# A convolution and a score layer on one core: each load cut in two and put behind a quarter of the output, on one queue

## The chip, the cores and the metric

The kernel runs on one core of one Trainium2 chip. The metric is the time of one execution on the device in microseconds (us); of several runs the median is given.

## The reference

Two layers on `x` of shape (4, 64, 256, 256), in float32. Batch is `b`, channel `c`, and each of the 256 (batch, channel) images is 256 x 256.

```python
# layer 0: a long convolution in two dimensions, whose kernel is an outer product
k = einsum('ijk,imk->ijmk', hx, hy)[0]       # hx, hy: small sine networks times a decay, (1, 256, 64)
k = transpose(k, (2, 0, 1))                  # one 256 x 256 kernel per channel, of rank one
y = irfft2(rfft2(x, s=(512, 512)) * rfft2(k, s=(512, 512)) / 512, s=(512, 512))[..., :256, :256]
x = y + x * bias[:, None, None]

# layer 1: weighted scores of the rows with each other, then a normalization per channel
scores = einsum('bpsd,bptd->bpst', x, x) / sqrt(256)
red = sum(scores * weights[None], axis=-1, keepdims=True)
y = x + red
y_hat = (y - mean(y, axis=(0, 2, 3))) * rsqrt(var(y, axis=(0, 2, 3)) + 1e-5)
out = y_hat * gamma[None, :, None, None] + beta[None, :, None, None]
```

## The kernel before

The work is one loop over the 64 channels; one pass of it handles all four images of a channel and is called a period here. The convolution kernel is of rank one, so the convolution is done as two multiplications with Toeplitz matrices, one along each axis. `toep` holds both Toeplitz matrices of a channel. The four images of a channel stand side by side as 64 x 64 blocks, so that every matmul uses a quarter of the array (64 rows, 64 columns).

The stages of a channel, by function:

- `conv_rows(c, u)` (matmuls on line L165) multiplies half `u` of `xin`, the input in the order that this product needs, with `toep`; it fills two PSUM tiles. `copy_rows` (L174, ScalarE, here ACT) copies them to `z`.
- `conv_cols(c, z)` (matmuls L189) makes the second product. VectorE (DVE) adds `x * bias` from `xt`, a second copy of the input in the output's order, and writes `x0` (L196).
- `gram(c, v)` (matmuls L221) makes the scores of two images. `weigh` (L234, L238) multiplies them with the weights `w` and sums; `spread` (L245, ACT) and `all_sum` (L250 on DVE, then L251, a sum over all partitions on GpSimd, here POOL) bring the row sums into the layout of `x0`. `pick_red` (L258, ACT) and `add_red` (L263, DVE) add them.
- `part_stats` and `stats` (L270, L276, L279) take mean and variance, `root` (L285 to L292) the standard deviation on ACT and POOL, `scale_shift` (L296 to L304, DVE) the factor and the offset.
- `finish` (L312, ACT) applies them and stores the result.

The order of the instructions on each engine is the order in which the program is written (`manual_schedule`). The main loop is software-pipelined: pass `c` works on `conv_cols` and `gram` of channel `c`, on `conv_rows` of `c + 1`, on `all_sum` and `add_red` of `p = c - 1`, on the statistics of `q = c - 2`, and on `finish` of `f = c - 3`.

All loads are issued on the queue of SyncE (SP): at the head of pass `c` come `load_w(c + 2)` (256 KB, L73), `load_xt(c + 2)` (1 MB, L68), `load_x(c + 3)` (1 MB, L63) and `load_h(c + 3)` (two DMAs of 128 KB for `toep`, L136, which wait until `conv_cols(c)` has read the buffer). The stores are issued on the queue of ACT, two of 512 KB in a period, each right behind its activation (L313). Load buffers are threefold (pool `ld`), `o` twofold, `x0` fourfold.

Before the loop a small network on 128 partitions makes `hx` and `hy` of all channels (L109 to L125); the result is written to DRAM (`g_dram`), from where `load_h` reads the Toeplitz matrices. The loads of channels 0 to 2 are issued around this.

On PE each matmul is preceded by its own weight load (PEld in the profile), both from one instruction stream.

## Time and profile before

| | |
|---|---|
| Three runs | 1023.18, 1023.28, 1025.0 us; median 1023.28 |
| Profiled execution | 1023.52 us; span from first to last instruction 1021.7 us |
| TensorE matmul (PE) busy | 923.9 us, 90%, 21,512 instructions |
| Weight loads (PEld) busy | 822.4 us, 80%, 21,512 instructions |
| DVE / ACT / POOL busy | 782.5 us (77%) / 519.5 us (51%) / 441.9 us (43%) |
| DMA | 238.70 MB, mean 234 GB/s; queue q1 (SP) 51.1%, q10 (ACT) 16.8% of 16 engines' time |
| Mean granted TensorE clock | 0.986 |

The profile is of one execution. An engine's busy time is the time in which one of its instructions ran; a line number such as L189 is a line of the kernel, and `x<-xt,p` says which tile is written from which. The chain that ended last follows the work back from the last instruction, at each step to what released it. "Issue" is time in which an engine stood still although the profile shows nothing that it waited for. A wait is listed as who waited, for what, the total in us, how often, and the longest. Stretches ("windows") give the busy time of each engine between two moments. A queue's share is the time that its packets took, over the time of all 16 DMA engines.

### The profile page before, as it was taken

The page shows a single profiled execution, that of the slowest core. Times are in us where ns is not written, and L with a number is a line of the kernel's source. Part 1 is how long each engine was busy: PE and PEld are TensorE (multiplying, and loading weights), DVE is VectorE, ACT ScalarE, POOL GpSimd, SP SyncE. Part 2 cuts the span into 40 slices and gives each one's busy share as a digit, 9 for nine tenths or more (in the row PEclk, how much of TensorE's full clock was granted, in tenths as well). Part 3 has the DMA queues.
Part 4 walks back from the last instruction along what each step waited for, and adds up shares of the span by engine and source line. Part 5 has one row for each costly group of instructions (what it writes and reads, how often), then busy time and mean ns, then how long its engine had stood idle before and what let it go on. Part 6 is the DMA issues. An engine that isn't in the chain of part 4 may idle for free.

```text
span 1021.7 us, 47771 instructions
## 1 busy us (share of the span) xinstructions
PE 923.9 (90%) x21512; PEld 822.4 (80%) x21512; DVE 782.5 (77%) x1878; ACT 519.5 (51%) x1029; POOL 441.9 (43%) x196
## 2 busy tenths in 40 slices
PE   2999999999999989999999999999999999999980
PEld 1888889898888978888878888889888888888870
DVE  2368778887777977887878787788787888778794
ACT  0245455455455545555545555545554554554554
POOL 0045345345345535534534543544453454454353
PEclk9999999999999999999999999999999999999995
DMA  7667587677577768677767677867776876776523
GB/s 209 192 199 253 204 270 246 227 255 267 202 259 237 260 231 283 233 243 260 249 208 270 223 246 259 276 226 242 274 238 212 279 246 218 265 241 246 190 85 123
DMA packets 65699, 238.70 MB, mean 234 GB/s; under 512 B 7446, under 2 KB 24536, under 8 KB 49112
## 3 DMA queue, kind: packets, MB, share of 16 engines
q1 hardware_dynamic: 46284, 167.89, 51.1%
q10 hardware_dynamic: 19212, 67.76, 16.8%
q8 instruction: 169, 2.77, 1.1%
q14 instruction: 34, 0.28, 0.1%
HBM read 168.05 MB, written 67.31 MB: 230 GB/s over the span
## 4 chain that ended last, share of the span: by engine, by line
PE 89%; issue 5%; DVE 3%; DMA 1%; POOL 1%; ACT 1%; POOLq 0%; ACTq 0%; DVEq 0%
PE g L221 34%; PE p L189 28%; PE p L165 27%; DMA toep<-g_sb 1%; POOL rd L251 1%; DVE x L263 0%; DVE bst L270 0%; PE ph L109 0%; DVE junk L234 0%; DVE x L196 0%; DVE fa L118 0%; ACT o L312 0%; DVE pr L238 0%; DMA fw_sb<-in_fw 0%; DVE fa L111 0%
## 5 line engine op out<-in xcount | busy, mean ns | idle before, releaser
L251 POOL PARTITION_ALL_REDUCE rd<-sp x64 | 391.8, 6122 | 425.3 <-DVE r L296 366.1
L221 PE MATMUL g<-x 64*64 64x256 f32 (+1 forms) x8192 | 376.2, 325 | 39.9 <-issue 38.1
L221 PEld LDWEIGHTS g<-x 64*64 64x64 f32 x8192 | 320.0, 133 | 82.7 <-issue 54.6
L165 PEld LDWEIGHTS p<-toep,xin 64*64 64x64 f32 x8192 | 296.5, 134 | 27.3 <-issue 12.4
L165 PE MATMUL p<-toep,xin 64*64 64x256 f32 (+3 forms) x8192 | 309.1, 298 | 10.1 <-DMA toep<-g_sb 7.3
L189 PE MATMUL p<-z,toep 64*64 64x256 f32 x5120 | 306.9, 377 | 8.0 <-issue 7.7
L189 PEld LDWEIGHTS p<-z,toep 64*64 64x64 f32 x5120 | 241.9, 133 | 47.0 <-issue 13.7
L234 DVE SCALAR_TENSOR_TENSOR junk<-g,w 128x256 f32<-128x256 f32 x256 | 107.1, 418 | 179.7 <-PE g L221 179.4
L312 ACT ACTIVATE o<-x,sh,g 128x1024 f32<-128x1024 f32 x128 | 159.0, 1242 | 149.3 <-DVE sh L304 122.3
L245 ACT ACTIVATE sp<-eye_sb,red 128x128 f32<-128x128 f32 x256 | 98.0, 397 | 202.5 <-DVE junk L234 202.0
L196 DVE SCALAR_TENSOR_TENSOR x<-xt,chan_sb,p 128x512 f32<-128x512 f32 x256 | 173.8, 740 | 19.4 <-PE p L189 19.4
L174 ACT COPY z<-p 128x512 f32<-128x512 f32 x256 | 136.2, 591 | 89.0 <-PE p L165 72.1
L270 DVE BATCH_NORM_STATS2 bst<-x 128x6 f32<-128x512 f32 x256 | 157.8, 678 | 0.0
L263 DVE TENSOR_TENSOR x<-x,rd 128x1024 f32<-128x1024 f32 x128 | 150.5, 1217 | 3.1 <-ACT rd L258 3.1
L238 DVE SCALAR_TENSOR_TENSOR pr<-g,w 128x256 f32<-128x256 f32 x256 | 107.6, 420 | 0.0
L288 POOL PARTITION_ALL_REDUCE tot<-mv x64 | 25.3, 396 | 119.2 <-ACT mv L287 119.2
L250 DVE TENSOR_TENSOR sp<-pr 128x512 f32<-128x512 f32 x64 | 44.3, 692 | 2.2
L258 ACT COPY rd<-rd 64x512 f32<-64x512 f32 x64 | 39.3, 615 | 5.8 <-POOL rd L251 4.3
L279 POOL PARTITION_ALL_REDUCE tot<-mv x64 | 24.7, 386 | 26.7 <-DVE mv L276 26.7
L290 ACT ACTIVATE r<-tot,eps 128x1 f32<-128x1 f32 x64 | 18.9, 295 | 32.8 <-POOL tot L288 32.8
L287 ACT ACTIVATE mv<-d,mv 128x1 f32<-128x1 f32 x64 | 24.8, 387 | 2.1
L299 DVE TENSOR_SCALAR u<-v,r 128x1 f32<-128x1 f32 x64 | 17.5, 273 | 7.0
(31 smaller groups left out, 161.6 us busy)
## 6 DMA issues: line engine op xcount, KB each, us to landing
xin<-in_x SPq DMA_DIRECT2D x64, 1024.0 KB, 9.7
xt<-in_xT SPq DMA_DIRECT2D x64, 1024.0 KB, 5.5
out<-o ACTq DMA_DIRECT2D x128, 512.0 KB, 8.5
w<-in_wl SPq DMA_DIRECT2D x64, 256.0 KB, 2.7
toep<-g_dram SPq DMA_DIRECT2D x126, 128.0 KB, 10.1
fw_sb<-in_fw ACTq DMA_DIRECT2D x1, 192.0 KB, 2.7
g_dram<-g_sb SPq DMA_DIRECT2D x1, 192.0 KB
decay_sb<-in_decay ACTq DMA_DIRECT2D x1, 128.0 KB, 5.6
```

What stands on the lines that cost most here:

```text
L165: nc.tensor.matmul(p1[i][half, j, H * k :], lhsT=xin[rows, k, u, j, half], rhs=toep[rows, 0, : S - H * k], start=(k == 0), stop=(k == 3),)
L174: nc.scalar.copy(zs[c][:, 2 * i : 2 * i + 2, u, :], p1[i])
L189: nc.tensor.matmul(p2[v][bass.ts(u, H), n, :], lhsT=toep[rows, 1, bass.ts(i - j, H)], rhs=z[rows, j, u, :], start=(j == 0), stop=(j == i),)
L196: nc.vector.scalar_tensor_tensor(x0[:, v, part], xt[:, v, part], chan_sb[:, 0, c : c + 1], p2[v], ALU.mult, ALU.add,)
L221: nc.tensor.matmul(gs[u][bass.ts(h, H), cols, :], lhsT=x0[rows, v, i, first + H * h : first + H * h + H], rhs=x0[rows, v, i, first:], star ...
L234: nc.vector.scalar_tensor_tensor(junk, g[:, 0:2, :], 1.0 / math.sqrt(S), w[:, 0:2, :], ALU.mult, ALU.mult, accum_out=red0[:, b : b + 1],)
L238: nc.vector.scalar_tensor_tensor(pr[:, b], g[:, 1:3, :], 1.0 / math.sqrt(S), w[:, 2:4, :], ALU.mult, ALU.mult)
L245: nc.scalar.activation(sp[:, b, 0, :], eye_sb, AF.Identity, scale=red0[:, b : b + 1])
L251: nc.gpsimd.partition_all_reduce(rd.rearrange("p b s -> p (b s)"), sp.rearrange("p b k s -> p (b k s)"), P, RED.add)
L263: nc.vector.tensor_tensor(x0[:, v], x0[:, v], r, ALU.add)
L270: nc.vector.bn_stats(bst[:, 2 * m + h, :], x0[:, m, 2 * h : 2 * h + 2])
L312: nc.scalar.activation(o[:, v], st8[c][0][:, v], AF.Identity, bias=sh, scale=g)
```

## The change

- `xin` and `xt` become two tiles each, with a DMA of 512 KB each; the arrays in DRAM are laid out so that each half is contiguous.
- The output is made in four parts per channel: `finish` handles one (128 x 512 elements), and each is stored with a DMA of 256 KB, on SP's queue and no longer on ACT's. The output array's layout follows; `o` has four buffers of a quarter.
- The four parts are put at four places of the period on ACT: ahead of `conv_cols`, between the two halves of `conv_rows`, between the two halves of the old `root` (now `spreads` and `root`), and after `gram(c, 0)`.
- Behind each store SP issues a load: a half of `xin`; the other half and `toep`; a half of `xt`; the other half and `w`. `xt` is loaded three channels ahead and no longer two.

The instructions of PE, DVE and POOL, and their order, stay as they are.

```diff
-    def load_x(c):
-        xin = ld.tile([P, 4, 2, 2, P], F32, tag="xin", name=f"xin_{c}")
-        nc.sync.dma_start(xin, x[c])
-        xs[c] = xin
+    def load_x(c, u):
+        xin = ld.tile([P, 4, 2, P], F32, tag=f"xin{u}", name=f"xin_{c}_{u}")
+        nc.sync.dma_start(xin, x[c, u])
+        xs[c, u] = xin
...
-    def root(c, mv, tot):
+    def spreads(c, mv, tot):
...
         nc.gpsimd.partition_all_reduce(tot[:, 1:2], mv[:, 2:3], P, RED.add)
+        return d
+
+    def root(c, tot):
+
         r = sm.tile([P, 1], F32, tag="r", name=f"r_{c}")
...
-    def finish(c, g, sh):
-        o = wk.tile([P, 2, 4, S], F32, tag="o", name=f"o_{c}")
-        for v in range(2):
-            nc.scalar.activation(o[:, v], st8[c][0][:, v], AF.Identity, bias=sh, scale=g)
-            nc.scalar.dma_start(out[c, :, v], o[:, v])
+    def finish(c, g, sh, v, n):
+        part = bass.ts(n, 2)
+        o = wk.tile([P, 2, S], F32, tag="o", name=f"o_{c}_{v}_{n}", bufs=4)
+        nc.scalar.activation(o, st8[c][0][:, v, part], AF.Identity, bias=sh, scale=g)
+        nc.sync.dma_start(out[c, v, n], o)
...
     for c in range(C + 3):
         p, q, f = c - 1, c - 2, c - 3
-        if c + 2 < C:
-            load_w(c + 2)
-            load_xt(c + 2)
-        if c + 3 < C:
-            load_x(c + 3)
-            load_h(c + 3)
         if 0 <= p < C:
             spread(p, 2)
             spread(p, 3)
             all_sum(p)
         if f >= 0:
-            finish(f, *scale_shift(f, *scales.pop(f)))
+            fin = (f, *scale_shift(f, *scales.pop(f)))
+            finish(*fin, 0, 0)
+        if c + 3 < C:
+            load_x(c + 3, 0)
         if c < C:
             begin(c)
             conv_cols(c, zs.pop(c))
         if 0 <= q < C:
-            sums[q] = stats(q, part_stats(q))
+            mv, tot = stats(q, part_stats(q))
         if c + 1 < C:
             begin_rows(c + 1)
-            for u in range(2):
-                copy_rows(c + 1, u, conv_rows(c + 1, u))
+            copy_rows(c + 1, 0, conv_rows(c + 1, 0))
+        if f >= 0:
+            finish(*fin, 0, 1)
+        if c + 3 < C:
+            load_x(c + 3, 1)
+            load_h(c + 3)
+        if c + 1 < C:
+            copy_rows(c + 1, 1, conv_rows(c + 1, 1))
         if 0 <= p < C:
             pick_red(p)
         if 0 <= q < C:
-            scales[q] = root(q, *sums.pop(q))
+            d = spreads(q, mv, tot)
+        if f >= 0:
+            finish(*fin, 1, 0)
+        if c + 3 < C:
+            load_xt(c + 3, 0)
+        if 0 <= q < C:
+            scales[q] = (d, *root(q, tot))
         if c < C:
             gram(c, 0)
             spread(c, 0)
             spread(c, 1)
+        if f >= 0:
+            finish(*fin, 1, 1)
+        if c + 3 < C:
+            load_xt(c + 3, 1)
+        if c + 2 < C:
+            load_w(c + 2)
         if 0 <= p < C:
             add_red(p, 0)
             add_red(p, 1)
```

`load_xt` is cut as `load_x` is; the loads before the loop follow (`x` and `xt` of channels 0 to 2 in halves, `xt` of channel 2 now before the loop).

More of the change, by code (lines that the diff above doesn't have):

```diff
@@ L59, in conv_scores_bn_kernel, with load_xt @@
     xs, xts, ws, hs = {}, {}, {}, {}
-    def load_x(c):
-        xin = ld.tile([P, 4, 2, 2, P], F32, tag="xin", name=f"xin_{c}")
-        nc.sync.dma_start(xin, x[c])
-        xs[c] = xin
-    def load_xt(c):
-        xt = ld.tile([P, 2, 4, S], F32, tag="xt", name=f"xt_{c}")
-        nc.sync.dma_start(xt, xT[c])
-        xts[c] = xt
+    def load_x(c, u):
+        xin = ld.tile([P, 4, 2, P], F32, tag=f"xin{u}", name=f"xin_{c}_{u}")
+        nc.sync.dma_start(xin, x[c, u])
+        xs[c, u] = xin
+    def load_xt(c, v):
+        xt = ld.tile([P, 4, S], F32, tag=f"xt{v}", name=f"xt_{c}_{v}")
+        nc.sync.dma_start(xt, xT[c, v])
+        xts[c, v] = xt
     def load_w(c):
@@ L95, in conv_scores_bn_kernel @@
     nc.vector.memset(g_sb[:, :P], 0.0)
-    load_x(0)
-    load_xt(0)
-    load_w(0)
-    load_x(1)
-    load_xt(1)
+    for c in range(2):
+        load_x(c, 0)
+        load_x(c, 1)
+        load_xt(c, 0)
+        load_xt(c, 1)
+        if not c:
+            load_w(c)
     g_dram = dram.tile([P, GW], F32, name="g_dram")
@@ L155, in conv_rows @@
     def conv_rows(c, u):
-        xin, toep = xs[c], hs[c]
+        xin, toep = xs.pop((c, u)), hs[c]
         p1 = [ps.tile([P, 2, S], F32, tag="ps", name=f"p1_{c}_{u}_{i}") for i in range(2)]
@@ L166, in conv_rows @@
                         p1[i][half, j, H * k :],
-                        lhsT=xin[rows, k, u, j, half], rhs=toep[rows, 0, : S - H * k],
+                        lhsT=xin[rows, k, j, half], rhs=toep[rows, 0, : S - H * k],
                         start=(k == 0), stop=(k == 3),
@@ L176, in conv_cols @@
     def conv_cols(c, z):
-        xt, toep, x0 = xts.pop(c), hs.pop(c), st8[c][0]
-        xs.pop(c)
+        xt = [xts.pop((c, v)) for v in range(2)]
+        toep, x0 = hs.pop(c), st8[c][0]
         for m in range(2):
@@ L196, in conv_cols @@
                 nc.vector.scalar_tensor_tensor(
-                    x0[:, v, part], xt[:, v, part], chan_sb[:, 0, c : c + 1], p2[v],
+                    x0[:, v, part], xt[v][:, part], chan_sb[:, 0, c : c + 1], p2[v],
                     ALU.mult, ALU.add,
@@ L292, in root @@
         nc.scalar.activation(v, tot[:, 1:2], AF.Identity, bias=eps, scale=1.0 / P)
-        return d, v, r
+        return v, r
     def scale_shift(c, d, v, r):
@@ L307, in scale_shift @@
         return g, sh
-    def finish(c, g, sh):
-        o = wk.tile([P, 2, 4, S], F32, tag="o", name=f"o_{c}")
-        for v in range(2):
-            nc.scalar.activation(o[:, v], st8[c][0][:, v], AF.Identity, bias=sh, scale=g)
-            nc.scalar.dma_start(out[c, :, v], o[:, v])
+    def finish(c, g, sh, v, n):
[3 more added lines that the diff above has]
+        nc.sync.dma_start(out[c, v, n], o)
     load_h(1)
     load_w(1)
-    load_x(2)
+    load_x(2, 0)
+    load_x(2, 1)
     load_h(2)
+    load_xt(2, 0)
+    load_xt(2, 1)
     def begin_rows(c):
@@ L401 @@
     arrays = {
-        "x": xi.transpose(2, 5, 4, 3, 0, 6, 1, 7).reshape(C, P, 4, 2, 2, P),
-        "xT": xo.transpose(2, 0, 5, 1, 4, 3).reshape(C, P, 2, 4, S),
+        "x": xi.transpose(2, 0, 5, 4, 3, 6, 1, 7).reshape(C, 2, P, 4, 2, P),
+        "xT": xo.transpose(2, 1, 0, 5, 4, 3).reshape(C, 2, P, 4, S),
         "wl": wl,
@@ L420 @@
     ]
-    o = nc.dram_tensor("out", (C, P, 2, 4, S), F32, kind="ExternalOutput").ap()
+    o = nc.dram_tensor("out", (C, 2, 2, P, 2, S), F32, kind="ExternalOutput").ap()
     with tile.TileContext(nc) as tc:
@@ L424 @@
     r = run_bass_kernel_spmd(nc, [arrays], core_ids=[0])
-    y = r.results[0]["out"].reshape(C, 2, H, 2, 4, S)
-    return np.ascontiguousarray(y.transpose(1, 3, 0, 5, 4, 2).reshape(B, C, S, S))
+    y = r.results[0]["out"].reshape(C, 2, 2, 2, H, 2, S)
+    return np.ascontiguousarray(y.transpose(3, 1, 0, 6, 2, 5, 4).reshape(B, C, S, S))
```

## The prediction

> **What bounds the kernel now.** I read the chain that ended last first, then TensorE's waits, then stretches of one channel each, then single waits in the timeline, then the DMA queues.

> ```profile
> ## 4 chain that ended last, share of the span: by engine, by line
> PE 89%; issue 5%; DVE 3%; DMA 1%; POOL 1%; ACT 1%; POOLq 0%; ACTq 0%; DVEq 0%
> ```

> ```profile
> PE g L221 <- issue: 38.1, 41, 2.4
> ...
> PE p L189 <- issue: 7.7, 15, 1.1
> ...
> PE p L165 <- issue: 2.7, 3, 1.0
> ```

> The end is set by PE. The second item is no other engine but "issue": PE stood still for nothing that a semaphore explains, 59 times, 48.5 us. No load, DVE or ACT wait of weight stands beside it.

> Stretches from the first L189 matmul of one channel to that of the next (columns: length, busy time of each engine, granted clock, DMA share, GB/s):

> ```profile
> 75.86:89.74 13.88, 13.88 (x347) 11.28 (x343) 12.08 (x30) 8.17 (x17) 6.89 (x3) 1.00 0.71 242
> 380.52:394.40 13.88, 13.88 (x344) 12.91 (x340) 11.53 (x29) 8.00 (x16) 6.89 (x3) 1.00 0.77 260
> 559.64:576.89 17.25, 14.34 (x344) 13.32 (x340) 12.02 (x30) 8.22 (x16) 6.89 (x3) 1.00 0.63 217
> 968.39:982.27 13.88, 13.88 (x344) 13.37 (x340) 12.17 (x30) 7.90 (x16) 6.89 (x3) 1.00 0.20 79
> ```

> The same 344 or so matmuls take 13.88 us wherever PE does not stop, with heavy DMA traffic and with little: 13.88 is the floor of the period. DVE has 1.8 us and ACT 5.7 us to spare in it. The first L189 matmul starts at 31.13 and that of the last channel at 982.27: 63 periods in 951.14 us, 15.10 each. So 63 x (15.10 - 13.88), or 76.5 us, lie above the floor (some 2 us of it in one stretch, 89.74 to 108.13, where the granted clock was 0.91 after a stop).

> The stops in the bad stretch, and what the queues carried (start, length, operation):

> ```profile
> 561.19 3.83 PE L189 MATMUL p<-z,toep 64*64 64x256 f32 x65 [0.51 <-issue]
> ...
> 574.23 2.05 PE L221 MATMUL g<-x 64*64 64x128 f32 x34 [2.40 <-issue]
> ```

> ```profile
> 562.75 1.31 SPq L68 DMA_DIRECT2D xt<-in_xT  x1
> 564.16 0.38 SPq L63 DMA_DIRECT2D xin<-in_x  x1
> ```

> ```profile
> 565.63 0.34 ACTq L313 DMA_DIRECT2D out<-o  x1
> ...
> 567.29 0.34 ACTq L313 DMA_DIRECT2D out<-o  x1
> ```

> ```profile
> q1 hardware_dynamic: 46284, 167.89, 51.1%
> q10 hardware_dynamic: 19212, 67.76, 16.8%
> q8 instruction: 169, 2.77, 1.1%
> ...
> out<-o ACTq DMA_DIRECT2D x128, 512.0 KB, 8.5
> w<-in_wl SPq DMA_DIRECT2D x64, 256.0 KB, 2.7
> ```

> Queue q8 is the key. It carries 169 packets of 16,384 bytes, and PE runs 43,024 loads and matmuls plus 319 semaphore instructions: 256 instructions to a packet. So q8 brings PE its program. In the trace's own records PE stops for over 0.3 us 69 times between 45 and 960 us, 70.5 us in all, every time at the same place modulo 256 instructions, and resumes 0.97 to 1.62 us (median 1.36) after a q8 packet ended. PE runs out of instructions because the next block arrives late.

> Why late: after a stop the next block's packet starts at the earliest 1.04 us after PE enters a block; it takes 0.98 us (median); PE can go on 1.36 us later: 3.38 us. A block lasts 5.21 us (median). So a fetch may queue for some 1.8 us before PE stops. The data ahead of it is longer: w, xt and xin are issued within 2 us, the stores 1.5 and 3.1 us later. A 8,192-byte packet takes 0.309 us and 16 engines get 8 each per 1 MB, so xt and xin alone are 4.9 us of work on every engine; the stores, issued at 565.63 and 567.29, move nothing of note before 569.5, and land after 8.5 us where w needs 2.7. The late fetch of this stretch started at 571.74, when the loads had drained.

> **The change, part by part.** *Loads and stores cut and spread.* Instead of one bunch (0.7 us of w, 4.9 of loads, 0.7 of toep, 2.5 of stores per engine), SP issues four: store+xin, store+xin+toep, store+xt, store+xt+w. With a 4,096-byte packet at 0.159 us and a 2,048-byte one at 0.084, they are 8 x 0.084 + 8 x 0.159 = 1.9; 1.9 + 0.7 = 2.7; 1.9; and 1.9 + 0.7 = 2.6 us. Each waits for its ACT part, so from the rows of ACT they come some 4.2, 8.3, 12.1 and 14.2 us into the period: all but the last two have time to drain. A fetch then meets at most about 2.7 us, and stops PE only if it finds over 1.8: the time with more than 1.8 us outstanding is about 0.1 + 0.9 + 0.1 + 0.8 = 1.9 us of 13.88, some 14%; allowing a third more for packets that are slowed by each other, 19%, with a mean excess of 0.5. At 2.65 fetches per period and 63 periods that is 0 to 16 us; PE's sequencer also runs ahead, which hides part, so I take 7. The cut itself makes the packets dearer: 32 x 0.159 for 16 x 0.309 and 32 x 0.084 for 16 x 0.159, +0.3 us per period on an engine, total 9.1 of 13.88: hidden, and if the DMA were the bound it would be 63 x 0.3 = 19 us.

> [...]

> *Stores move from ACT's queue to SP's.* ACT loses 2 x 0.34 us of issue, and gets four activations of 512 columns for two of 1,024 (1,242 ns). A 512-column one lies between 0.62 (half) and 0.76 (on the line through 128 columns, 397 ns): +0.0 to +0.6 us per period, under 5.7 to spare. The part between the two copies of z runs while PE does the other half of conv_rows (2.1 us); the part between spreads and root fills the 0.51 us wait for POOL; that behind the first two spreads ends by about 14.2, before DVE's L196 at 3.5 of the next period needs the slot. Cost: nothing; uncovered it is at most 63 x 0.6 = 38 us.

> *SP becomes one line of eleven transfers.* Behind a store that waits for ACT stand loads, and behind load_h, which waits for conv_cols, the third store. The loads are read 20 us or more later, over a period ahead. In the order of the changed kernel each transfer also waits for the landing of the eighth before it, about 10 us earlier; the longest median landing today is 10.1, in the bunch that goes away. Eleven issues of 0.33 to 0.62 are 5 of 13.88 us. Cost: nothing, unless SP lags by over a period.

> *More waits.* PE gets one more wait per channel (the second half of xin), DVE one. By the 38 ns of a semaphore instruction (ACT's row L312) that is 0 to 2.4 us on PE; its sequencer runs ahead, so I take 0.

> *Ends.* At the start the first matmul waits for toep_0 with the same bytes before it: 0, bounds -1 to +1. At the end four activations take 2.5 to 3.0 us for 1.24 + 0.42 + 1.24 = 2.9, and the last store is half as large (0.67 us less): -0.5, bounds -1.1 to 0.

> **Sum**, against the profiled execution's 1023.52 us (span 1021.70, 1.8 around it; the median of the runs is 0.24 lower): 1023.5 - 76.5 + 7 - 0.5 = 953.5 us.

> **Rivals.**
> *All stops vanish.* If a fetch is served between two transfers, it waits for one load piece at most, 8 x 0.159 = 1.27 us, under 1.8: 946.5 us. For it: some fetches start amid load packets (81.69 us, with 15 engines on loads). Against: the fetch at 571.74 outwaited two loads. [...] 12%.

> *Half the stops stay*, since the last two bunches run together (12.1 to 17) and contention stretches packets: 1023 - 70.5/2 - 2 = 986 us. For it: load packets average more than their 0.309 in the bunch. 14%.

> *Slower.* Today 91 of 160 blocks escape, since the queues fall quiet for 3 to 5 us per period; traffic spread over the period could catch every fetch. If each waited behind a whole piece pair of 2.6 us, PE would stop 2.6 - 1.8 = 0.8 us at each of 160 blocks: 128 us for 70.5, 1081 us. It decides from a mean stop of 70.5/160 = 0.44 us per block, a mean queueing of 2.2 us. Against: the pieces need only 9.1 of 13.88 us, and a fetch finds on average a half-drained one. 9%.

> *It does not spread.* If SP falls behind its ACT waits, the pieces run in one bunch again: 1023 us. Against: ACT's slack. 3%.

> **The numbers.** The forecast has 62%, and 946 to 962 is its own range. All but the last two cases are faster: 0.88; the same (within 0.2%, about what runs from 1023.18 to 1025.0 can tell) 0.03; slower 0.09. The range reaches from the floor less the bounds of the ends, 945, to the half case, 985, which holds 62 + 12 + half of 14.

> **What would show it.** Right: "issue" in TensorE's waits falls below some 10 us, most stretches are 13.88, and q8 still has 169 packets; store landings fall from 8.5 to under 5; no new wait of PE on xin or of DVE on xt. Wrong: stops that stay at the 256-instruction places (partial or slower rival), or PE waiting for loads, or DVE's L196 waiting for ACT's last part.

## The result and the profile after

The changed kernel took 964.41 us in the median of four runs (960.04 to 969.80), the kernel before 1023.23 us (1019.99 to 1025.0): a ratio of 0.9431 with a 95% interval of 0.9376 to 0.9486. The forecast was 953.5 us, with a range of 945 to 985; its own narrower range, 946 to 962, is missed by 2.4 us. The profiled execution is the slowest of the four, 969.80 us with a span of 967.9. Of the experiments, spread_only's profile is of the slowest of its four runs (1081.06 us, clock 0.968), which its ratio leaves out as a run in a slower state, so the sizes of its waits are read with care.

The chain and TensorE's waits of the changed kernel:

```profile
## 4 chain that ended last, share of the span: by engine, by line
PE 92%; DVE 3%; issue 2%; DMA 1%; POOL 1%; ACT 1%; ACTq 0%; DVEq 0%; POOLq 0%
```

```profile
PE p L167 <- issue: 11.0, 10, 5.3
...
PE p L191 <- issue: 4.0, 4, 2.1
PE g L223 <- issue: 2.4, 3, 1.4
```

"Issue" fell from 48.5 to 17.4 us; 5.3 of these are one wait at the start, before the first channel. In the gram matmuls (L221 before, L223 now) it went from 38.1 to 2.4.

Stretches from the first matmul of one channel's `conv_cols` to that of the next (length, busy time of each engine, granted clock, DMA share, GB/s):

```profile
162.29:176.17 13.88, 13.88 (x345) 13.08 (x340) 12.08 (x30) 8.36 (x19) 6.89 (x3) 1.00 0.84 267
275.68:289.56 13.88, 13.88 (x345) 11.30 (x341) 12.08 (x30) 8.36 (x19) 6.89 (x3) 1.00 0.92 271
417.52:432.62 15.10, 14.26 (x344) 13.07 (x340) 12.01 (x30) 8.08 (x19) 6.90 (x3) 1.00 0.75 242
```

The floor of 13.88 us is unchanged, and 35 of the 63 stretches are on it, for 8 before, even with the DMA engines 92% busy. In the third one PE still stops once:

```profile
420.68 2.60 PE L191 MATMUL p<-z,toep 64*64 64x256 f32 x43 [0.84 <-issue]
```

The 63 stretches take 899.7 us, 14.28 each, for 951.1. The start is 1.9 us shorter (the first L191 matmul at 29.2 us) and the end 0.4: 1023.5 - 51.4 - 1.9 - 0.4 = 969.8 us, the profiled time.

The queues, and the transfers' time from issue to landing:

```profile
q1 hardware_dynamic: 101580, 235.03, 78.6%
q8 instruction: 169, 2.77, 1.2%
...
xin<-in_x SPq DMA_DIRECT2D x128, 512.0 KB, 4.7
xt<-in_xT SPq DMA_DIRECT2D x128, 512.0 KB, 6.2
out<-o SPq DMA_DIRECT2D x256, 256.0 KB, 3.9
w<-in_wl SPq DMA_DIRECT2D x64, 256.0 KB, 6.7
toep<-g_dram SPq DMA_DIRECT2D x126, 128.0 KB, 5.6
```

The same 169 instruction packets come in; the stores land after 3.9 us for 8.5. But w lands after 6.7 us for 2.7: behind the last two parts of the output a queue still stands.

### The profile page after: what moved, and what is told of

It reads as the page before. It is cut to its first block, busy times and chain, and to the rows that moved or that the text cites. A ratio compares the mean times of both kernels' runs of the same rounds, so it can differ in the third digit from the quotient of the medians.

```text
span 967.9 us, 48479 instructions
## 1 busy us (share of the span) xinstructions
PE 908.3 (94%) x21512; PEld 845.4 (87%) x21512; DVE 781.5 (81%) x1878; ACT 539.8 (56%) x1157; POOL 442.2 (46%) x196
## 3 DMA queue, kind: packets, MB, share of 16 engines
q8 instruction: 169, 2.77, 1.2%
## 4 chain that ended last, share of the span: by engine, by line
PE 92%; DVE 3%; issue 2%; DMA 1%; POOL 1%; ACT 1%; ACTq 0%; DVEq 0%; POOLq 0%
PE g L223 34%; PE p L167 29%; PE p L191 29%; DMA toep<-g_sb 1%; POOL rd L253 1%; DVE x L265 1%; DVE bst L272 0%; PE ph L111 0%; DVE junk L236 0%; DVE x L198 0%; DVE fa L120 0%; DVE pr L240 0%; ACT o L318 0%; DMA zT_sb<-in_zT 0%; DVE fa L113 0%
## 5 line engine op out<-in xcount | busy, mean ns | idle before, releaser
L223 PE MATMUL g<-x 64*64 64x256 f32 (+1 forms) x8192 | 359.7, 323 | 3.9 <-issue 2.4
L223 PEld LDWEIGHTS g<-x 64*64 64x64 f32 x8192 | 325.9, 133 | 24.6 <-issue 5.3
L167 PEld LDWEIGHTS p<-toep,xin 64*64 64x64 f32 x8192 | 301.7, 134 | 27.0 <-issue 15.8
L167 PE MATMUL p<-toep,xin 64*64 64x192 f32 (+3 forms) x8192 | 312.4, 298 | 12.0 <-issue 11.0
L191 PE MATMUL p<-z,toep 64*64 64x256 f32 x5120 | 303.7, 376 | 4.5 <-issue 4.0
L191 PEld LDWEIGHTS p<-z,toep 64*64 64x64 f32 x5120 | 254.5, 133 | 29.4 <-issue 7.2
L318 ACT ACTIVATE o<-x,sh,g 128x512 f32<-128x512 f32 x256 | 207.2, 812 | 120.7 <-DVE sh L310 91.9
L247 ACT ACTIVATE sp<-eye_sb,red 128x128 f32<-128x128 f32 x256 | 95.8, 397 | 127.7 <-DVE junk L236 127.7
L236 DVE DVE_READ_ACCUMULATOR junk<-g,w 128x1 f32 x256 | 21.3, 83 | 0.0
## 6 DMA issues: line engine op xcount, KB each, us to landing
xin<-in_x SPq DMA_DIRECT2D x128, 512.0 KB, 4.7
xt<-in_xT SPq DMA_DIRECT2D x128, 512.0 KB, 6.2
out<-o SPq DMA_DIRECT2D x256, 256.0 KB, 3.9
w<-in_wl SPq DMA_DIRECT2D x64, 256.0 KB, 6.7
```

Source lines behind the costliest of these rows:

```text
L167: nc.tensor.matmul(p1[i][half, j, H * k :], lhsT=xin[rows, k, j, half], rhs=toep[rows, 0, : S - H * k], start=(k == 0), stop=(k == 3),)
L191: nc.tensor.matmul(p2[v][bass.ts(u, H), n, :], lhsT=toep[rows, 1, bass.ts(i - j, H)], rhs=z[rows, j, u, :], start=(j == 0), stop=(j == i),)
L223: nc.tensor.matmul(gs[u][bass.ts(h, H), cols, :], lhsT=x0[rows, v, i, first + H * h : first + H * h + H], rhs=x0[rows, v, i, first:], star ...
L236: nc.vector.scalar_tensor_tensor(junk, g[:, 0:2, :], 1.0 / math.sqrt(S), w[:, 0:2, :], ALU.mult, ALU.mult, accum_out=red0[:, b : b + 1],)
L247: nc.scalar.activation(sp[:, b, 0, :], eye_sb, AF.Identity, scale=red0[:, b : b + 1])
L318: nc.scalar.activation(o, st8[c][0][:, v, part], AF.Identity, bias=sh, scale=g)
```

## The experiments

In the diffs, lines that only follow from the shown ones are left out. "Stops" are the pauses of PE of over 0.3 us in the trace's records between 45 and 960 us that fall at the same place modulo 256 instructions. The last column is an estimate of what the prediction reasoned with: the share of the time between 100 and 900 us in which more than 1.8 us of work per DMA engine had been issued and not yet started. It is worked out from the issue times (an issue counts once it is over and 0.85 us old, my estimate of the lag on an idle queue: in the kernel before the first packet of w starts 0.63 us after its issue, in the median) and the packet records, with each packet at its median time. Packet means and shares of busy engines below are of the same 100 to 900 us.

| Kernel | Median us | Ratio to before, 95% interval | Stops in the profiled run | Time with over 1.8 us waiting |
|---|---|---|---|---|
| before | 1023.23 | 1 | 69 | 59% |
| changed | 964.41 | 0.9431 (0.9376 to 0.9486) | 24 | 29% |
| before_no_loads | 952.55 | 0.9279 (0.9224 to 0.9335) | 6 | 9% |
| after_no_toep | 949.66 | 0.9245 (0.9192 to 0.9299) | 2 | 12% |
| cut_only | 1017.23 | 0.9929 (0.9891 to 0.9967) | 64 | 59% |
| spread_only | 1066.05 | 1.0345 (1.0253 to 1.0437) | 66 | 40% |
| spread_act_stores | 1039.16 | 1.0107 (1.0037 to 1.0178) | 63 | 57% |
| after_act_stores | 1040.92 | 1.0143 (1.0088 to 1.0198) | 65 | 58% |
| paced_act_stores | 970.53 | 0.9473 (0.9410 to 0.9535) | 17 | 31% |
| after_toep_apart | 988.40 | 0.9644 (0.9590 to 0.9697) | 41 | 33% |
| after_toep_copy | 964.13 | 0.9403 (0.9368 to 0.9439) | 22 | 29% |
| late_fourth | 992.78 | 0.9682 (0.9617 to 0.9746) | 37 | 27% |
| late_fourth_apart | 970.75 | 0.9465 (0.9405 to 0.9525) | 24 | 19% |
| late_fourth_copy | 959.59 | 0.9364 (0.9310 to 0.9418) | 15 | 20% |

Each ratio is to runs of the kernel before in the same session. The four kernels at 57% and more have 63 to 69 stops, the two at 9 and 12% have 6 and 2. But spread_only, whose transfers are not cut, has 66 at 40%, and late_fourth 37 at 27%: the work that waits goes with the stops, and is not all.

### Is it the data traffic that makes PE stop? (before_no_loads)

```diff
     def load_x(c):
+        if c >= 3:
+            xs[c] = kept["x", c % 3]
+            return
...
     def load_xt(c):
+        if c >= 3:
+            xts[c] = kept["xt", c % 3]
+            return
```

> The kernel before, in which from channel 3 on xin and xt are not loaded (the tiles of channels 0 to 2 are read again); w, toep and the stores go on. Theory A (PE stops because the fetch of its next 256 instructions queues behind data): 4.9 us of work per engine and period are gone, the stops too; the period falls to 13.88 us and the time to 946 to 955 us, with the same 169 packets on q8. Rival B (the stops belong to PE's program or to the fetch itself, whatever the data traffic): issue stays near 48 us and the time near 1023 us.

Measured: 952.55 us, and TensorE's waits for "issue" are

```profile
PE g L228 <- issue: 2.7, 4, 0.9
PE p L196 <- issue: 0.2, 1, 0.2
```

2.9 us for 48.5, with q8's 169 packets and with PE's instructions and their order untouched. Theory A holds, rival B falls: the program can be fetched in time, and it is the loads that make the fetch late.

### Which part of the change does it? (cut_only, spread_only, after_act_stores, spread_act_stores, paced_act_stores)

cut_only: the changed kernel's parts, all issued at the head of the pass, the stores on ACT's queue, and eight buffers of `o` for four.

```diff
+        if c + 2 < C:
+            load_w(c + 2)
+            load_xt(c + 2, 0)
+            load_xt(c + 2, 1)
+        if c + 3 < C:
+            load_x(c + 3, 0)
+            load_x(c + 3, 1)
+            load_h(c + 3)
...
-            finish(*fin, 0, 0)
+            for v in range(2):
+                for n in range(2):
+                    finish(*fin, v, n)
```

> Loads and stores in the parts of the changed kernel, but all at the head of the pass and on the queues of before (stores on ACT's). Theory A (what counts is the work outstanding when a fetch comes): the bunch is as long as before, the time 1010 to 1030 us. Rival C (a fetch is served between two transfers, so the size of a part counts): 955 to 975 us.

Measured: 1017.23 us, within A's range. Cutting alone brings 0.7% of the 5.7, and 64 of the stops stay.

spread_only: the loads and stores of before, whole, on SP's queue at two places of the pass, with toep between them.

```diff
+            finish(*fin, 0)
+        if c + 3 < C:
+            load_x(c + 3)
...
+        if c + 3 < C:
+            load_h(c + 3)
...
+            finish(*fin, 1)
+        if c + 3 < C:
+            load_xt(c + 3)
+        if c + 2 < C:
+            load_w(c + 2)
```

> Loads of 1 MB and stores of 512 KB, not cut further, but spread on SP's queue: store and xin at the head of the pass, toep behind conv_rows, store, xt and w ahead of gram. Two bunches of 3.7 and 5.1 us per engine for one of 8.8. Theory A: about half of what the change brings or more, 965 to 995 us. Rival C (size of a part): no better than 1010 us.

Measured: 1066.05 us, slower than before, which neither theory had. TensorE's waits:

```profile
PE g L221 <- issue: 66.9, 40, 3.4
PE p L165 <- issue: 13.6, 18, 1.6
PE p L189 <- issue: 7.2, 6, 2.1
```

The stops are as many as before (66), but longer: 40 of them in the gram matmuls make 66.9 us, where 41 made 38.1. By the packet records a bunch (store, xin, toep) is some 6 us of unbroken work on one queue, and after a stop the next fetch starts up to 6.1 us after PE has entered its block, for 3.75 at most in the kernel before. After long stops the granted clock also fell: the runs of the ratio have 0.973 and 0.974, for 0.986 in the profiled run of before. In the trace it is 0.5 for 3.4 us at a time, thirteen times while PE works, where the kernel before has this once. So two bunches of 6 us were worse than one of 11. That each can catch a fetch, and for longer than the 1.8 us to spare, is a reading that fits; no run tests it alone.

after_act_stores: the changed kernel with its stores on ACT's queue, everything else in place.

```diff
-        nc.sync.dma_start(out[c, v, n], o)
+        nc.scalar.dma_start(out[c, v, n], o)
```

> The changed kernel with its stores issued on ACT's queue, at the same places. Theory A (only the work outstanding on an engine counts, whatever queue it is on): 955 to 970 us, as the changed kernel. Rival D (one queue in alternation matters, because a fetch waits for what stands on one queue, or because SP's loads no longer wait for the parts of the output and run together): 975 us or more, or under 952 us if two queues serve the fetch sooner.

Measured: 1040.92 us. This one line takes away all of the gain and more. "And more" is mostly clock: the 63 stretches take 967.9 us, 16.7 more than before; 6.6 of these are longer stops, and the other some 10 (16.7 less 6.6), by an estimate, come from the granted clock, which is 0.5 for 3.4 us seven times while PE works, each behind a stop of over 2.2 us, and once in the kernel before (where 50 gram matmuls fell in 3.35 us of it, and 84 and 87 in two such stretches at full clock). What SP waits for shows why the gain is gone; the changed kernel first, then this one:

```profile
SPq L319 <- ACT o L318: 403.0, 190, 11.6
SPq L319 <- ACT v L298: 94.1, 59, 5.7
```

```profile
SPq L138 <- PE p L191: 333.1, 61, 9.7
SPq L138 <- DMA xt<-in_xT: 259.6, 57, 6.1
```

In the changed kernel SP stands before its stores, once for each part of the output, and so the loads come one by one. Without the stores SP stands before load_h, for conv_cols to read the old toep and for an earlier xt to land, and hardly elsewhere; then toep, both halves of xt, w and both halves of xin go out one behind the other, within 5.3 us in the median. In the packet records the unbroken stretches of traffic (at least six engines at work, pauses under 0.3 us joined) are 12.1 us long in the median (10.9 before). The loads are written at four places, but on an instruction stream that waits for nothing between them they leave as one bunch.

paced_act_stores: 7/8 of each store on ACT's queue, and 1/8 on SP's, ahead of each load.

```diff
-        nc.sync.dma_start(out[c, v, n], o)
+        nc.scalar.dma_start(out[c, v, n][:P - 16], o[:P - 16])
+        nc.sync.dma_start(out[c, v, n][P - 16 :], o[P - 16 :])
```

> The changed kernel with 7/8 of each store on ACT's queue and 1/8 on SP's, so that SP still waits for each part of the output before it issues the next load. With all of the store on ACT's queue, and SP not held, the time was 1040.9 us. Theory P (what counts is that SP is held until each part is done, so that loads cannot run ahead in one bunch; which queue moves the bytes is of no account): 955 to 975 us. Rival D (one queue serves the fetch sooner than two): 1000 us or more.

Measured: 970.53 us, with two queues that carry

```profile
q1 hardware_dynamic: 72908, 176.31, 63.0%
q10 hardware_dynamic: 33548, 59.38, 17.5%
```

SP is held again, and the gain is back, whichever queue moves the bytes. Theory P holds, rival D falls: "on one queue" matters only since a store there holds the loads behind it. Nor is it unbroken traffic that stops PE: the stretches are 11.9 us here, no shorter than before, with 17 stops for 69.

spread_act_stores is spread_only with the stores on ACT's queue.

```diff
-        nc.sync.dma_start(out[c, :, v], o)
+        nc.scalar.dma_start(out[c, :, v], o)
```

> Spread but not cut, as the run that took 1066 us, with the stores on ACT's queue. Theory A (outstanding work on the engine, whatever the queue): 1050 to 1075 us, the same. Rival D (it was slower than before because stores and loads share one queue, so that a fetch waits for all of it): 1000 to 1035 us.

Measured: 1039.16 us, between the two expectations. Here SP is no longer held by the output either (it waits 564.3 us for conv_cols ahead of load_h), so the run changed two things at once and does not separate the queue from the hold.

### What stayed above the forecast? (after_no_toep, after_toep_apart, after_toep_copy)

after_no_toep: from channel 3 on toep isn't loaded.

```diff
     def load_h(c):
+        if c >= 3:
+            hs[c] = kept[c % 3]
+            return
```

> The changed kernel, in which from channel 3 on toep is not loaded (the tiles of channels 0 to 2 are read again). Theory A1 (what stayed above the forecast, some 18 us, comes from toep, whose packets take 135 ns in the mean in the changed kernel for 51 before, so that the last two bunches run together): 948 to 955 us. Rival A2 (it comes from loads and stores, whose packets slow each other): 960 us or more.

Measured: 949.66 us with 2 stops: the floor. The stops that were left in the changed kernel depend on toep, 256 KB of the 3.5 MB of a period.

```profile
q1 hardware_dynamic: 84012, 219.03, 68.4%
```

q1's share falls by 10 points for 7% of its bytes. In the packet records a packet of toep, 1,024 bytes, takes 135 ns in the mean in the changed kernel (46 in the median), 51 before, and 130 in before_no_loads, where next to no loads run. So other traffic is not what makes it slow. In the changed kernel a toep packet that started while no load or store packet ran took 195 ns in the mean, one beside more than ten of them 78; in the kernel before 9,651 of the 15,616 toep packets started beside more than ten store packets of the other queue and took 48. The run takes away SP's two issues and 0.12 of the engines' time at once, so it does not show that the slowness of these packets, and not the room that they leave, is what counts.

after_toep_apart: toep's second DMA behind the third part.

```diff
-            load_h(c + 3)
+            load_h(c + 3, (0,))
...
+            load_h(c + 3, (1,))
             load_xt(c + 3, 0)
```

> The changed kernel with the second DMA of toep moved from behind the second store to behind the third. Without toep the time was 949.7 us for 964.4. Theory A1 (toep's slow packets join the bunches): half of toep then stands in front of xt, where the traffic is densest: 955 to 975 us, no clear gain. Rival A3 (it is the length of one bunch, store + xin + toep, that stops PE): 950 to 958 us.

Measured: 988.40 us, worse than either theory. In front of xt half of toep costs 24 us.

after_toep_copy: as that, with the second half copied within SBUF.

```diff
+            if vs == (1,):
+                src = toep[:H]
             nc.sync.dma_start(toep[bass.ts(v, H)], src)
```

> The changed kernel in which only one half of toep is read from DRAM and the other half is copied from it within SBUF, behind the third store (the two halves are the same). Theory A1 (reading toep costs 2.1 us per engine and period, 0.8 by its median packet, since so many rows are read from the same few places in DRAM): the work falls by 0.7 to 1 us per period and the time to 951 to 960 us. Rival A2 (its packets are slow because of the other traffic): the copied half is as slow, 960 us or more.

Measured: 964.13 us: 24 us less than after_toep_apart, no better than the changed kernel. The half that is still read from DRAM got cheap (67 ns a packet) and the engines' share of busy time fell from 0.85 to 0.80, some 0.8 us per period, as theory A1 had it; the time did not follow. Rival A2's range fits the time, but not its reason: the copied half lands after 2.3 us. The copy needs the first half's landing, and SP stands for that ahead of xt:

```profile
SPq L142 <- DMA toep<-g_dram: 132.9, 60, 7.2
```

### Can the parts be put better? (late_fourth, late_fourth_apart, late_fourth_copy)

In the changed kernel the parts start 4.9, 7.9, 11.8 and 13.4 us into the period in the median (the expectation has 4.2, 8.0, 11.8 and 13.6). late_fourth moves the last to the head of the next pass.

```diff
             all_sum(p)
+        if f >= 1:
+            finish(*fin, 1, 1)
+        if 0 <= c - 1 and c + 2 < C:
+            load_xt(c + 2, 1)
+        if 0 <= c - 1 and c + 1 < C:
+            load_w(c + 1)
...
-        if f >= 0:
-            finish(*fin, 1, 1)
-        if c + 3 < C:
-            load_xt(c + 3, 1)
-        if c + 2 < C:
-            load_w(c + 2)
```

> The changed kernel with the fourth part of the output, and the half of xt and w behind it, moved from the end of gram(c, 0) to the head of the next pass, behind the spreads. The parts then start about 1.5, 4.2, 8.0 and 11.8 us into the period for 4.2, 8.0, 11.8 and 13.6. Theory S (what stays above the floor comes from bunches that have no time to drain before the next): 950 to 960 us. Rival: it comes from toep behind the second part alone: 960 to 970 us, as the changed kernel.

Measured: 992.78 us, 37 stops: worse than either theory. The engines' work is the same (0.84 of the time, 0.85 in the changed kernel). The moved part started 2.8 us into the period in the median and not 1.5, only 2.0 us ahead of the next (the last two of the changed kernel: 1.7), so the run gave little of the room that was meant. Theory S's range is missed by far; whether room to drain counts is not settled by this run.

late_fourth_apart adds toep's second DMA behind the third part, as in after_toep_apart.

> As late_fourth, with the second DMA of toep behind the third part, where with the old places it cost 24 us (988.4 us). Theory S: the third part now has 3.6 us until the next, so the move no longer costs, and the longest bunch (store, xin, toep) is halved: 948 to 957 us. If toep in front of xt is bad whatever the room behind it: 970 us or more.

Measured: 970.75 us, in the range of the rival, whose reason it contradicts all the same: the move that cost 24 us at the old places gains 22 here. How a place does depends on what stands around it and, it seems, on where in the period the fetches fall; this was not settled.

late_fourth_copy copies one half behind the fourth part and puts w behind the third.

```diff
+        if 0 <= c - 1 and c + 2 < C:
+            load_h(c + 2, (1,))
+            load_xt(c + 2, 1)
...
+        if c + 2 < C:
+            load_w(c + 2)
```

> As late_fourth, with one half of toep copied within SBUF behind the fourth part, 7 us after the other half was issued (so that SP does not stand waiting for its landing, 133 us in the run that copied it behind the third part), and w behind the third part. Theory S with less work on the engines: 947 to 955 us, the best of all. Rival: SP or the copied half joins the bunch: 960 us or more.

Measured: 959.59 us, the lowest median of the full computation, above the expected 947 to 955; its interval (0.9310 to 0.9418) overlaps that of the changed kernel, so it is not shown to be faster. With

```profile
PE g L226 <- issue: 7.4, 9, 1.4
PE p L170 <- issue: 5.5, 2, 5.3
PE p L194 <- issue: 1.7, 2, 1.5
```

its 15 stops are what is left of "issue" behind the start, 9.3 us, and the fetch still comes late.

## Why the prediction was right, point by point

- **The cause** holds. PE stopped because its next 256 instructions came late behind data: without the loads 2.9 us of issue were left (before_no_loads), and without toep the changed kernel ran at the floor.
- **The floor** of 13.88 us holds: 35 stretches are on it, and none is below. No new bound appeared; DVE has 12.08 of 13.88 us.
- **The residual** was mis-sized. It was put at 7 us, bounds 0 and 16; in the profiled run the 63 stretches lie 899.7 - 874.7 = 25.0 us above the floor, 6.6 of it in the first three, where no output holds SP yet. The median run has some 20. The step that failed is the work per engine and period, put at 9.1 us. From the packet records it is 12 (0.85 of a period of 14.2): loads 6.1 for 5.1, toep 2.1 for 0.7, stores and w 3.5 for 3.4. I took each packet at its median, and the means are longer, for toep by far; the means of the kernel before would have given 10.7. So the bunches of "1.9 to 2.7 us" did not drain as meant: more than 1.8 us waited for 29% of the time (59% before), by the estimate of the table, for the 14 to 19% of the forecast, and w lands after 6.7 us. That the total still came within 11 us of the forecast is owed to the floor, which makes up most of it.
- **The spread by parts** worked for the reason given, each part waits for its ACT part, but I did not see that this wait is the change: I costed SP's waits at nothing, as something to be hidden. after_act_stores, without them, is at 1040.92 us.
- **Cutting** was argued as a smaller wait per fetch. Alone it gave 0.7%, and spreading alone cost 3.5%; only the two together, held, gave the gain.
- **ACT's part** was put between 0.62 and 0.76 us; it is outside:

```profile
L318 ACT ACTIVATE o<-x,sh,g 128x512 f32<-128x512 f32 x256 | 207.2, 812 | 120.7 <-DVE sh L310 91.9
```

  That is 4 x 0.81 for 2 x 1.24, +0.8 us per period, off the path as said (ACT is busy 8.4 of 13.88).
- **The ends**: -1.9 us at the start, past the bound of -1; -0.4 at the end, within -1.1 to 0. The last store was put 0.67 us shorter; by the prediction's own packet times it is 8 x 0.159 - 8 x 0.084 = 0.60.
- **The rivals**: the case in which all stops vanish fell (24 stay). The argument against it, that a late fetch outwaits the loads, does not hold in general: in the kernel before, eight or more load packets were running when the late fetch started in 32 of 61 cases, and 14 at 571.74, where I had read that the loads had drained. So a fetch gets in between load packets, but often later than the 1.8 us to spare: after a stop it starts up to 2.7 us later than at the earliest (3.75 less 1.04) in the kernel before, and, by an estimate, up to 5.1 (6.1 less the same 1.04) in spread_only, where one load is 8 x 0.309 = 2.5 us of work on an engine. The rival let a fetch wait for one load piece at most; after how many packets a fetch is served, no run shows. Halves of 512 KB cost the loads nothing on the engines: they took 6.2 us per engine and period in cut_only and 6.3 before.
- **The signs**: q8's 169 packets, stores below 5 us, no new wait of PE on xin came as said. Issue "below some 10 us" did not: 12.1 without the start. "Most stretches at 13.88" holds by a little (35 of 63). One wait was not foreseen: ACT waited 15 times, 28.9 us in all, for the store of the period before to leave its buffer; nothing of PE's waits follows from it.

Open: why moving the fourth part made more stops, why transfers that are spread but not cut stop PE so often, and why toep's packets are slow when they run alone. That so many of its rows overlap in DRAM is a guess that no run tested.

## What to carry to other kernels

When an engine stops for nothing that a semaphore explains, count its instructions between the stops: here a fixed number, 256, with all 69 stops of the kernel before at the same place, said that the program came late. It cost to have much data issued and waiting at once (more than 1.8 us of it for 59% of the time with 69 stops, for 29% with 24), even though the DMA engines were busy only 0.72 of the time. Long traffic without a break was not what cost (paced_act_stores: 11.9 us in the median, 17 stops), and pieces left whole cost time though less was waiting (spread_only: 1066.05 us at 40%, for 1023.23 at 59%). Spread the traffic by making the queue wait, not only by where the line stands in the program: here a load behind a store that waits for its data could not run ahead (paced_act_stores 970.53 us, after_act_stores without that wait 1040.92). Cost a transfer by the mean of its packets in the trace, not by the median (toep in the changed kernel: 135 ns and 46).
